# A planned transformer kernel: finer VectorE tasks and another weighing in the plan, and banded attention weights divided on GpSimd by sums from the exponentials

## The chip, the cores and the metric

One of the eight cores of a Trainium2 chip runs the whole program. The metric is the device time of one execution in microseconds (us). A core has TensorE (PE: matmuls, into PSUM), VectorE (DVE), ScalarE (ACT: activation functions from a loaded table), GpSimd (POOL, which works on SBUF alone) and SyncE (SP, which issues DMAs). Each engine runs its own instructions strictly in the order in which they were issued, and waits by semaphore where an operand isn't ready.

## The reference, cut to what matters

Two layers on x of 16 x 256 x 128 floats, all in float32. Layer 0 is softmax attention (stage A: 16 heads of 64) and a routed spline network (stage B). Layer 1 is a mix of linear attention and banded attention (stage C), then causal attention with normalised queries and keys and a mixture of 8 experts (stages D and E). A layernorm follows each. The part whose computation changes is the banded attention, 16 heads of 8, 65 offsets:

```python
s = jnp.einsum('bhsd,bhsd->bhs', qh, ks) * scale + rel_bias[off + WINDOW][None, :, None]
s = jnp.where(valid[None, None, :], s, -jnp.inf)
...
attn = jax.nn.softmax(scores, axis=0)
out, _ = jax.lax.scan(out_step, jnp.zeros_like(qh), (attn, jnp.arange(NWIN)))   # acc + a * vs
```

## The kernel before

The 4096 tokens are cut into 8 groups of 512 (two sequences, four tiles of 128). Each group passes the stages A to E. The code doesn't issue instructions as it walks through the stages: it hands tasks to `Plan.add`, each with its engine (or a choice: "VS" is VectorE or ScalarE), a cost in ns, the buffers that it reads and writes, and an `at`, the group's number plus the stage's offset (0 to 4). `Plan.order` then simulates the engines: again and again it lets that task begin next which can begin soonest, ties broken by `at`. Costs, a lag from one engine to another (`LAG`), a lag on the same engine (`OWN`), 1300 ns for a change of ScalarE's table (`SWITCH`) and 93 for a change of PE's tiling mode (`DRAIN`) are numbers in the code. Buffers come from the classes in `SLOTS`, so many of each; PSUM has four banks `p` and two double banks `s`. The instructions are issued in the order found, engine by engine. So the plan decides which stage of which group stands beside which.

The stages, with the lines of the profile:

- A and D take heads in pairs (`pair`): scores into an `s` bank (PE), the negated maximum (VectorE; line 616 in A; in D mask, two maxima and a scaling, 607, 612, 614), exponentials with their sums from ScalarE's accumulator (634), the reciprocal of the sums (641), the weights times it on GpSimd (647, in place, `pb`), transposes (PE, 662), a copy to `pt` on VectorE or ScalarE (531, 529), and the product with the values.
- B is a long chain of small VectorE instructions on 32 numbers a row, with few matmuls.
- C has, beside the linear attention, eight blocks a group of 64 queries and 96 or 128 keys. For each: the masked queries `qm` (GpSimd, 1031), scores of 16 heads into an `s` bank, bias and maximum (VectorE, 1064, 1065), eight exponentials (1076, `pbC`) without sums, transposes (1082), copies (`ptC`), and 32 matmuls of 64 columns: 16 with the values, spread so that each head has its own columns (`vm`), and 16 with a matrix of ones (`hones`), which give the sums over the keys in the same layout. VectorE then takes the reciprocal of the 64 sums (1109) and multiplies (1110).
- E has 8 experts: four matmuls `h,we` and GELUs each (1346, `hid`), 16 matmuls `we,hid`, and four gated sums into `moe` on VectorE (1361). GELU and exponential lie in different tables. GELUs come in bursts of two experts' (`NBURST`), in which no other ScalarE task with another burst may stand. One task fetches both weights of an expert (1337, 1338).
- A layernorm is three tasks: the statistics of the four tiles (540, 542, VectorE), the root (545, 549, GpSimd), and four scalings (553, VectorE). After stage E come a layernorm, three GpSimd products and sums (`affine`, 927), another layernorm and the DMA out (1368).

Many tasks hold several instructions of one engine, which then follow each other: the four gated sums, the mask, maxima and scaling of a causal pair, the twelve instructions of `rsqrt` (1152 to 1160).

Of the kernel before, what the change touches and what calls it, by code (L numbers as in the profile page):

```python
# [10 lines left out]
I32 = mybir.dt.int32  # L11
AF = mybir.ActivationFunctionType
# [34 lines left out]
    ("ov", 256, 8),  # L47
    ("m", 64, 26),
    ("k1", 256, 4),
    ("b", 512, 2),  # L50
    ("sc", 288, 1),
    ("c", 512, 8),
    ("qm", 512, 2),
    ("pbC", 512, 2),
# [5 lines left out]
    ("e", 512, 1),  # L60
    ("hid", 512, 5),
    ("we", 1024, 2),
# [20 lines left out]

class Plan:

    LAG = {"P": 270.0, "V": 150.0, "S": 170.0, "G": 120.0, "Q": 0.0, "D": 0.0}
    OWN = 80.0
    SWITCH = 1300.0  # L90
    DRAIN = 93.0

# [8 lines left out]
    def add(self, eng, cost, fn, r=(), w=(), at=None, table=None, burst=None, mode="f", hold=()):  # L101
# [9 lines left out]
        for objs, writes in ((r, False), (w, True)):  # L111
            for o in objs:
                o, part = o if isinstance(o, tuple) else (o, None)
                if isinstance(o, Buf):
                    bufs[id(o)] = o
                for q, (writers, readers) in self.state.setdefault(id(o), {}).items():
                    if part is None or q is None or q == part:
                        before.update(writers)
                        if writes:
                            before.update(readers)  # L120
# [23 lines left out]
    def order(self):  # L144
        free = {e: 0.0 for e in "PVSGQD"}
# [17 lines left out]
        while done < len(self.tasks):  # L163
            best = None
            avail = {c: sorted(x for x in v if x is not None) for c, v in slots.items()}
            for e, ts in cand.items():
                pick = None
                for t in ts:
# [3 lines left out]
                    for x, end in t.ready.items():  # L172
                        start = max(start, end + (self.OWN if x == e else self.LAG[x]))
# [65 lines left out]
def kernel(ctx: ExitStack, tc: tile.TileContext, a: dict, out: bass.AP):  # L239
# [231 lines left out]
    hones = ctile("hones", [P, 4, 4 * WD])  # L471

# [7 lines left out]
    def setup_consts():  # L480
# [9 lines left out]
        made((ready_c, "h"), 220, lambda: G.memset(hones, 0.0))  # L490
        for l in range(4):
            made((ready_c, "h"), 60, lambda l=l: G.memset(hones[:, l, l * WD : (l + 1) * WD], 1.0))
# [40 lines left out]
    def layernorm(o, z, name, after=()):  # L533

        mv, rs = W.buf("m", "mv" + name), W.buf("m", "rs" + name)

        def stats():
            st = mv()[:, 8 : 8 + NJ * 6].rearrange("p (j s) -> p j s", s=6)
            for j in range(NJ):
                nc.vector.bn_stats(st[:, j, :], z(J, d=D)[:, j, :])  # L540
            for j in range(NJ):
                nc.vector.bn_aggr(mv()[:, 2 * j : 2 * j + 2], st[:, j, :])

        def root():
            nc.gpsimd.tensor_scalar(
                rs()[:, NJ : 2 * NJ], mv()[:, 0 : 2 * NJ].rearrange("p (j s) -> p j s", s=2)[:, :, 1], EPS, 1.0,
                ALU.add, ALU.mult,
            )
            nc.gpsimd.tensor_tensor(out=rs()[:, 0:NJ], in0=rs()[:, NJ : 2 * NJ], in1=mhalf, op=ALU.pow)

        def scaled():
            for j in range(NJ):
                nc.vector.tensor_scalar(  # L553
                    o(J, d=D)[:, j, :], z(J, d=D)[:, j, :], mv()[:, 2 * j : 2 * j + 1], rs()[:, j : j + 1],
                    ALU.subtract, ALU.mult,
                )

        W.add("V", NJ * (195 + 70), stats, r=[z, *after], w=[mv])
        W.add("G", 1300, root, r=[mv], w=[rs])
        W.add("V", NJ * 257, scaled, r=[z, mv, rs], w=[o])  # L560

# [15 lines left out]
    def pair(pi, qT, kT, v, ov, causal, rq, un=0):  # L577
# [24 lines left out]
        def top():  # L602
            s = sps(S2, a=2)
            n = nmx(n=4, pattern="p (a b) -> p a b", a=2)
            if causal:
                diag = s[:, :, P : 3 * P].rearrange("p a (b k) -> p a b k", k=P)
                nc.vector.tensor_tensor(  # L607
                    out=diag, in0=diag, in1=cmask.unsqueeze(1).unsqueeze(1).to_broadcast([P, 2, 2, P]), op=ALU.add
                )
                for qc in range(2):  # L610
                    c0, nk = col[qc]
                    nc.vector.tensor_reduce(n[:, :, qc], s[:, :, c0 : c0 + nk], AX.X, ALU.max, negate=True)  # L612
                rqp = rq("p (b i m) -> p i m b", n=16, b=2, i=2)[:, pi, 2 * un : 2 * un + 2, :]
                nc.vector.tensor_tensor(out=n, in0=n, in1=rqp, op=ALU.mult)  # L614
            else:
                nc.vector.tensor_reduce(n, s.rearrange("p a (b k) -> p a b k", k=S), AX.X, ALU.max, negate=True)  # L616

        cost = 1790 if causal else dve(1024)
        W.add("V", cost, top, r=[rq] if causal else [], w=[sps, nmx])
# [207 lines left out]
    def stage_b(g):  # L827
# [82 lines left out]
        def add_up():  # L910
            for q, j in enumerate(order):
                V.scalar_tensor_tensor(
                    y(J, d=D)[:, j, :], pv()[:, q, 65:NPAR], mag()[:, q : q + 1], xx(J, d=D)[:, j, :], ALU.mult, ALU.add
                )

        W.add("V", 4 * 259, add_up, r=[pp, mag, xx], w=[y, end_b])
# [5 lines left out]
    def affine(y, gam, bet, xx):  # L922

        nJ = [P, NJ, D]
# [10 lines left out]
    def stage_c(g):  # L935
# [48 lines left out]
        for b in range(2):  # L984
# [24 lines left out]
            def divide(b=b, pn2=pn2, rden=rden):  # L1009
                r = rden()[:, :2]  # L1010
                V.tensor_scalar(r, pn2()[:, :, D], 1e-6, None, ALU.add)
                V.reciprocal(r, r)
                V.tensor_tensor(
                    out=lin(J, d=D)[:, 2 * b : 2 * b + 2, :], in0=pn2()[:, :, :D],
                    in1=r.unsqueeze(2).to_broadcast([P, 2, D]), op=ALU.mult,
                )

            W.add("V", 360 + dve(256), divide, r=[pn], w=[rden, (lin, b)])
# [3 lines left out]
            for i, (w0, w1_) in enumerate(win_of):  # L1022
# [39 lines left out]
                def top(sps=sps, nmx=nmx, nk=nk, t0=t0):  # L1062
                    s8 = sps("p (u k) -> p u k", u=8)[:, :, :nk]
                    V.tensor_tensor(out=s8, in0=s8, in1=band[:, :, t0 : t0 + nk], op=ALU.add)  # L1064
                    V.tensor_reduce(nmx()[:, :8], s8, AX.X, ALU.max, negate=True)  # L1065

                W.add("V", 130 + 2 * dve(8 * nk), top, w=[sps, nmx])
                pts = []
                for half in range(2):
                    pb, pt, tps = W.buf("pbC", "pbC"), W.buf("ptC", "ptC"), W.buf("p", "tpsC")  # L1070

                    def weigh(sps=sps, nmx=nmx, pb=pb, half=half, nk=nk):
                        s8 = sps("p (u k) -> p u k", u=8)
                        for u in range(4):
                            hp = 4 * half + u
                            act(pb("p (u k) -> p u k", u=4)[:, u, :nk], s8[:, hp, :nk], AF.Exp, bias=nmx()[:, hp : hp + 1])  # L1076

                    W.add("S", 4 * (146 + 0.81 * nk), weigh, r=[sps, nmx], w=[pb], table="exp")
# [10 lines left out]
                def values(po=po, pts=pts, vm=vm, nk=nk):  # L1089

                    for what in range(2):
                        for l in range(4):
                            for j in range(4):
                                r = slice(32 * j, 32 * j + 32)
                                h = 4 * j + l
                                c = ((h // 2) % 4) * P + (h % 2) * QC
                                mm(
                                    po()[r, what * QC : (what + 1) * QC],
                                    hones[:nk, l, :] if what else vm[:nk, l, r],
                                    pts[j // 2]()[:nk, c : c + QC],  # L1100
                                    start=l == 0,
                                    stop=l == 3,
                                )

                W.add("P", 1200, values, r=[vt] + pts, w=[po, chain_c[2]], hold=[winT], mode="c32")
                rw = W.buf("m", "rw")

                def divide(po=po, rw=rw, c0=c0):
                    V.reciprocal(rw()[:, :QC], po()[:, QC : 2 * QC])
                    V.tensor_tensor(out=winT()[:, c0 : c0 + QC], in0=po()[:, :QC], in1=rw()[:, :QC], op=ALU.mult)  # L1110

                W.add("V", 700, divide, r=[po], w=[rw, (winT, (b, i))])
# [33 lines left out]
    def rsqrt(o, x, n, eps):  # L1146
# [3 lines left out]
        def go():  # L1150
            V = nc.vector
            V.tensor_scalar(ve(n=n), x(n=n), eps, None, ALU.add)
            yi = y(n=n).bitcast(I32)
            V.tensor_scalar(yi, ve(n=n).bitcast(I32), 1, None, ALU.logical_shift_right)
            V.tensor_scalar(yi, yi, -1.0, float(0x5F3759DF), ALU.mult, ALU.add)
            for k in range(3):
                src, dst = (y, o) if k % 2 == 0 else (o, y)
                V.tensor_mul(u(n=n), src(n=n), src(n=n))
                V.scalar_tensor_tensor(u(n=n), u(n=n), -0.5, ve(n=n), ALU.mult, ALU.mult)
                V.scalar_tensor_tensor(dst(n=n), u(n=n), 1.5, src(n=n), ALU.add, ALU.mult)  # L1160

        W.add("V", 2465 + 12 * (n - 16), go, r=[x], w=[ve, y, u, o])

    def stage_d(g):
# [9 lines left out]
        def half(b, hf):  # L1174
# [13 lines left out]
            for u in range(2):  # L1188
# [12 lines left out]
                def keep(e, ps_q=ps_q, qT=qT, u=u):  # L1201
                    for i in range(2):
# [7 lines left out]
                W.add("VS", (782, 714), keep, r=[ps_q], w=[qT])  # L1210
# [109 lines left out]
    def stage_e(g):  # L1320
# [4 lines left out]
        n = NJ * NE  # L1325
        tg, gT, pb2, moe = W.buf("p", "tg"), W.buf("k1", "gT"), W.buf("p", "pb2"), W.buf("e", "moe")
# [89 lines left out]
```

## Time and profile before

| | |
|---|---|
| median of 3 runs | 2226.43 us (2225.33 to 2226.8) |
| the profiled execution's own time | 2226.4 us |
| its span, first to last instruction | 2224.7 us |
| TensorE busy | 2099.0 us, 94% |
| VectorE busy | 1663.4 us, 75% |
| ScalarE busy | 1308.8 us, 59% |
| GpSimd busy | 784.0 us, 35% |
| mean granted TensorE clock | 0.986 of full |
| ScalarE table loads | 59 of 1.283 us |

"Busy" is the union of an engine's instructions. Matmuls are pipelined, so one that lasts 0.28 us may be followed by the next after 0.11; where it matters, the distance from start to start is used. A stretch is read as start and end in us from the span's start, and a wait as who waited for whom: us in total, times, longest.

### The profile page before, as it was taken

What the parts mean: (1) busy time and instruction counts of PE and PEld (TensorE: products, weight loads), DVE (VectorE), ACT (ScalarE), POOL (GpSimd) and SP (SyncE); (2) the same over time, 40 slices, a digit from 0 to 9 for tenths busy, and PEclk for the clock granted to TensorE, in tenths of its full rate; (3) what the DMA queues carried; (4) which work ended last, traced back from release to release, by engine and by line L of the source; (5) the groups of instructions that cost most, each with busy time, mean ns of one, the idle gap of its engine ahead of it and who ended that gap; (6) DMA issues with size and microseconds to landing.
All of it is one profiled execution on the core that took longest, in us unless ns stands there. A gap on an engine that the chain in (4) does not pass through costs nothing.

```text
span 2224.7 us, 49747 instructions
## 1 busy us (share of the span) xinstructions
PE 2099.0 (94%) x18506; PEld 1563.7 (70%) x18506; DVE 1663.4 (75%) x4784; ACT 1308.8 (59%) x3817; POOL 784.0 (35%) x1413
## 2 busy tenths in 40 slices
PE   8999999999999998999999999999899989989987
PEld 6777777767767766776777767777667667766655
DVE  5788899886688965788757895788856984784742
ACT  4566666764667643676647664666545755654632
POOL 3444362452143621435304360243502530431311
PEclk9999999999999999999999999999999999999998
DMA  5100000000100001000010001100011001101101
GB/s 141 30 1 2 2 1 2 2 2 26 48 15 2 2 29 35 25 2 1 23 41 25 2 1 40 39 6 2 2 43 34 7 2 55 27 1 44 39 20 43
DMA packets 69490, 47.98 MB, mean 22 GB/s; under 512 B 12064, under 2 KB 59904, under 8 KB 69248
## 3 DMA queue, kind: packets, MB, share of 16 engines
q1 hardware_dynamic: 68672, 43.74, 7.3%
q8 instruction: 147, 2.41, 0.5%
q10 hardware_dynamic: 576, 1.05, 0.2%
q14 instruction: 95, 0.78, 0.1%
HBM read 41.89 MB, written 2.88 MB: 20 GB/s over the span
## 4 chain that ended last, share of the span: by engine, by line
PE 53%; DVE 20%; ACT 5%; POOL 2%; issue 2%; POOLq 0%; DVEq 0%; ACTq 0%
PE p L523 39%; PE s L523 6%; PE p L662 4%; DVE m L612 2%; ACT pb L634 2%; PE p L1082 2%; DVE s L607 2%; DVE m L540 1%; DVE m L616 1%; POOL pb L647 1%; DVE x L553 1%; DVE m L614 1%; PE p L1265 1%; DVE uq L1208 1%; DVE s L1064 1%
## 5 line engine op out<-in xcount | busy, mean ns | idle before, releaser
L647 POOL TENSOR_SCALAR pb<-pb,m 128x256 f32<-128x256 f32 (+1 forms) x1024 | 453.8, 460 | 766.9 <-DVE m L641 675.1
L1346 ACT ACTIVATE hid<-p,b 128x512 f32<-128x512 f32 x256 | 170.5, 688 | 304.7 <-PE p L523 290.4
L662 PE MATMUL p<-ident,pb 128*128 128x128 f32 x1792 | 290.0, 282 | 14.1 <-POOL pb L647 5.0
L634 ACT ACTIVATE pb<-s,m,m 128x128 f32<-128x128 f32 (+1 forms) x512 | 257.4, 522 | 61.5 <-DVE m L614 50.7
L634 ACT ACTIVATE pb<-s,m 128x256 f32<-128x256 f32 x512 | 238.8, 490 | 70.5 <-DVE m L616 59.4
L662 PEld LDWEIGHTS p<-ident,pb 128*128 128x128 f32 x1792 | 206.1, 142 | 102.0 <-POOL pb L647 46.8
L523 PE MATMUL p<-h,we 128*128 128x512 f32 x512 | 264.2, 617 | 9.5 <-ACT hid L1346 4.9
L523 PEld LDWEIGHTS p<-we,hid 128*128 128x128 f32 x2048 | 243.3, 194 | 29.9 <-issue 15.7
L523 PE MATMUL p<-we,hid 128*128 128x128 f32 x2048 | 252.8, 279 | 3.9 <-ACT hid L1346 2.1
L529 ACT COPY pt<-p 128x512 f32<-128x512 f32 (+1 forms) x316 | 168.6, 540 | 129.1 <-PE p L662 117.3
L1361 DVE SCALAR_TENSOR_TENSOR e<-p,m,e 128x128 f32<-128x128 f32 x256 | 71.9, 344 | 143.7 <-PE p L523 122.0
L616 DVE TENSOR_REDUCE m<-s 128x4 f32<-128x1024 f32 x128 | 154.7, 1217 | 15.7 <-PE s L523 14.5
L1255 POOL TENSOR_TENSOR kn<-kn,m 128x512 f32<-128x512 f32 x64 | 66.2, 1049 | 283.9 <-DVE m L1160 232.3
L1076 ACT ACTIVATE pbC<-s,m 128x96 f32<-128x96 f32 (+1 forms) x512 | 135.3, 382 | 33.8 <-DVE m L1065 29.3
L523 PE MATMUL s<-ua,ua 64*128 64x256 f32 x1024 | 139.4, 395 | 10.5 <-ACT pb L634 9.0
L523 PE MATMUL s<-ud,uq 64*128 64x128 f32 (+1 forms) x1024 | 118.0, 352 | 21.4 <-ACT pb L634 20.4
L523 PE MATMUL p<-pt,ua 128*64 128x256 f32 x1024 | 136.2, 388 | 1.7 <-ACT pt L529 1.3
L531 DVE COPY pt<-p 128x512 f32<-128x512 f32 (+1 forms) x196 | 120.9, 621 | 20.9 <-PE p L662 19.5
L612 DVE TENSOR_REDUCE m<-s 128x2 f32<-128x256 f32 (+1 forms) x256 | 130.8, 553 | 5.3
L523 PEld LDWEIGHTS p<-h,we 128*128 128x128 f32 x512 | 84.9, 193 | 64.4 <-issue 30.6
L1031 POOL TENSOR_TENSOR qm<-c,hm 128x512 f32<-128x512 f32 x64 | 68.1, 1070 | 153.4 <-PE s L523 132.8
L523 PEld LDWEIGHTS s<-ua,ua 64*128 64x128 f32 x1024 | 91.2, 187 | 39.5 <-ACT pb L634 14.3
(273 smaller groups left out, 4294.0 us busy)
## 6 DMA issues: line engine op xcount, KB each, us to landing
we<-in_L_ffn_w_dram SPq DMA_DIRECT2D x128, 256.0 KB, 2.8
x<-_attn_hidden_states_dram SPq DMA_DIRECT2D x8, 256.0 KB, 2.8
out_dram<-x SPq DMA_DIRECT2D x8, 256.0 KB, 2.3
dpad<-k SPq DMA_DIRECT2D x1, 768.0 KB, 10.3
wq<-in_L_attn_Wq_dram ACTq DMA_DIRECT2D x2, 256.0 KB
wkv<-in_L_attn_Wkv_dram ACTq DMA_DIRECT2D x2, 256.0 KB, 6.8
wkv<-in_L_attn_Wkv_dram SPq DMA_DIRECT2D x2, 256.0 KB, 5.6
wo<-in_L_attn_Wo_dram SPq DMA_DIRECT2D x1, 512.0 KB, 8.4
```

Of the source, the lines that this page charges most:

```text
L523: nc.tensor.matmul(o, lhsT=lhsT, rhs=rhs, start=start, stop=stop)
L529: nc.scalar.copy(o, i)
L531: nc.vector.tensor_copy(o, i)
L612: nc.vector.tensor_reduce(n[:, :, qc], s[:, :, c0 : c0 + nk], AX.X, ALU.max, negate=True)
L616: nc.vector.tensor_reduce(n, s.rearrange("p a (b k) -> p a b k", k=S), AX.X, ALU.max, negate=True)
L634: act(pb()[:, c0 : c0 + nk], s[:, par, c0 : c0 + nk], AF.Exp, bias=nmx()[:, 2 * par + qc : 2 * par + qc + 1], accum_out=sums()[:, 2 * par ...
L647: eng.tensor_scalar(pb()[:, c0 : c0 + nk], pb()[:, c0 : c0 + nk], sums()[:, 2 * par + qc : 2 * par + qc + 1], 1.0, ALU.mult, ALU.mult,)
L662: nc.tensor.transpose(tps()[:, at * P : (at + 1) * P], pb()[:, c0 + kc * P : c0 + (kc + 1) * P], ident)
L1031: (V if e == "V" else G).tensor_tensor(out=qm("p (h q) -> p h q", q=QC), in0=qw()[:, c0 : c0 + QC].unsqueeze(1).to_broadcast(nq), in1=hm8. ...
L1076: act(pb("p (u k) -> p u k", u=4)[:, u, :nk], s8[:, hp, :nk], AF.Exp, bias=nmx()[:, hp : hp + 1])
L1346: W.add("S", 571, lambda ph=ph, hid=hid, ec=ec: act(hid(), ph(), AF.Gelu_apprx_tanh, bias=b1[:, ec : ec + 1]), r=[ph], w=[hid], table="gel ...
L1361: V.scalar_tensor_tensor(m, pe_()[:, j * D : (j + 1) * D], gate()[:, j * NE + e_ : j * NE + e_ + 1], m, ALU.mult, ALU.add)
```

## The change

It has two parts.

The banded weights. Each of the eight exponentials of a block now also writes the sum of its row (`accum_out`). A reciprocal of four sums on VectorE and a product on GpSimd (`pbC` by the reciprocals, four heads at once) divide the weights before they are transposed. The 16 matmuls with ones, the matrix `hones`, the reciprocal of 64 columns and the product behind them are gone; the result is copied from PSUM by VectorE or ScalarE.

The plan. Tasks that held several VectorE instructions are cut into one task each: layernorm statistics and scalings, the causal maxima, the sums of stage B, the division of the linear attention, `rsqrt`, the gated sums. A part of a buffer may now be named by kind, so that parts of different kinds are taken to overlap (`overlap`). `order` computes for each task the longest chain of work behind it, divides it by a weight, takes it off the task's `at`, runs the old procedure (now `line`) with each of ten weights, and keeps the plan whose simulated end is soonest. The lags and some costs have new values. The weights of an expert are fetched by two tasks into buffers of their own. A first GELU matmul of a group now comes after the sum of b2 (`begun`). For the last group alone, the two layernorms and the affine step go tile by tile, the affine step on VectorE, with a DMA out for each tile. Some classes of buffers have a slot more or fewer.

```diff
-    ("ov", 256, 8), ("m", 64, 26), ("k1", 256, 4), ("c", 512, 8), ("qm", 512, 2), ("pbC", 512, 2),
-    ("e", 512, 1), ("hid", 512, 5), ("we", 1024, 2),
+    ("ov", 256, 7), ("m", 64, 30), ("k1", 256, 5), ("c", 512, 7), ("qm", 512, 1), ("pbC", 512, 3),
+    ("e", 512, 2), ("hid", 512, 6), ("w1", 512, 2), ("w2", 512, 2),
...
-    LAG = {"P": 270.0, "V": 150.0, "S": 170.0, "G": 120.0, "Q": 0.0, "D": 0.0}
-    OWN = 80.0
+    LAG = {"P": 265.0, "V": 178.0, "S": 200.0, "G": 60.0, "Q": 0.0, "D": 0.0}
+    OWN = {"P": 0.0, "V": 130.0, "S": 80.0, "G": 80.0, "Q": 0.0, "D": 0.0}
+    RESTS = (1e5, 8e4, 6e4, 5e4, 4e4, 3e4, 2.5e4, 2e4, 1.5e4, 1e4)
...
     def order(self):
+        rest = {}
+        for t in reversed(self.tasks):
+            rest[t.seq] = min(t.cost) + max([self.LAG[t.eng[0]] + rest[n.seq] for n in t.then], default=0.0)
...
+        def again(weight):
+            for t, t.wait, at in first[0]:
+                t.ready, t.end, t.at = {}, None, at - rest[t.seq] / weight
...
+        return again(min(ends)[1])
...
-                            act(pb("p (u k) -> p u k", u=4)[:, u, :nk], s8[:, hp, :nk], AF.Exp, bias=nmx()[:, hp : hp + 1])
+                            act(pb("p (u k) -> p u k", u=4)[:, u, :nk], s8[:, hp, :nk], AF.Exp, bias=nmx()[:, hp : hp + 1],
+                                accum_out=sm()[:, u : u + 1])
+                    W.add("V", 73, lambda sm=sm: V.reciprocal(sm()[:, :4], sm()[:, :4]), w=[sm])
+                    def share(pb=pb, sm=sm, nk=nk):
+                        w4 = pb("p (u k) -> p u k", u=4)[:, :, :nk]
+                        G.tensor_tensor(out=w4, in0=w4, in1=sm()[:, :4].unsqueeze(2).to_broadcast([P, 4, nk]), op=ALU.mult)
+                    W.add("G", gps(4 * nk), share, r=[sm], w=[pb])
...
-                    for what in range(2):
-                                    hones[:nk, l, :] if what else vm[:nk, l, r],
+                            mm(po()[r, :QC], vm[:nk, l, r], pts[j // 2]()[:nk, c : c + QC], start=l == 0, stop=l == 3)
...
-                    V.reciprocal(rw()[:, :QC], po()[:, QC : 2 * QC])
-                    V.tensor_tensor(out=winT()[:, c0 : c0 + QC], in0=po()[:, :QC], in1=rw()[:, :QC], op=ALU.mult)
+                    lambda e, po=po, c0=c0: copy(e, winT()[:, c0 : c0 + QC], po()[:, :QC]), r=[po], w=[(winT, (b, i))],
...
-        W.add("VS", (dve(512), scl(512)), lambda e: copy(e, moe(), pb2()), r=[pb2], w=[moe])
+        W.add("VS", (dve(512), scl(512)), lambda e: copy(e, moe(), pb2()), r=[pb2], w=[moe, begun])
...
-        layernorm(moe, moe, "E1")
-        affine(moe, lngb, lnbb, xx)
-        layernorm(xx, moe, "E2")
+        last = g == NG - 1
+        layernorm(moe, moe, "E1", own=last)
+        affine(moe, lngb, lnbb, xx, own=last)
+        if last:
+            layernorm(moe, moe, "E2", own=True)
```

## The prediction

> **What bounds the kernel now.** I read the page's busy times first, then busy times by stretches of the span, then the waits of TensorE (PE), then its timeline.
>
> ```profile
> span 2224.7 us, 49747 instructions
> ...
> PE 2099.0 (94%) x18506; PEld 1563.7 (70%) x18506; DVE 1663.4 (75%) x4784; ACT 1308.8 (59%) x3817; POOL 784.0 (35%) x1413
> ```
>
> TensorE is busy for all but 125.7 us (2224.7 - 2099.0). About 5.6 of these lie before its first matmul and 15.9 after its last, so some 104 us are gaps on the way. VectorE (DVE) at 75% looks harmless, but 75% is a mean. I cut the span at the first and last gated sum (line 1361) of every group, so that rows alternate between a stage E and what lies between two of them:
>
> ```profile
> core 0: us, PE busy (x) PEld busy (x) DVE busy (x) ACT busy (x) POOL busy (x), PEclk, DMA share, GB/s
> 0.00:530.90 530.90, 507.27 (x4600) 387.14 (x4601) 440.79 (x1189) 324.50 (x1056) 231.80 (x442) 1.00 0.09 20
> 530.90:611.70 80.80, 79.69 (x573) 58.79 (x571) 47.38 (x153) 41.15 (x81) 8.29 (x14) 1.00 0.16 47
> 611.70:803.30 191.60, 183.27 (x1762) 136.59 (x1761) 161.16 (x442) 123.63 (x404) 91.91 (x164) 0.98 0.02 7
> ...
> 1720.40:1839.70 119.30, 106.88 (x1128) 78.98 (x1127) 106.80 (x333) 73.93 (x221) 55.24 (x86) 0.97 0.03 8
> ...
> 2087.30:2157.90 70.60, 61.31 (x411) 41.66 (x410) 47.65 (x151) 38.95 (x122) 30.26 (x61) 0.93 0.03 8
> 2157.90:2209.90 52.00, 49.91 (x278) 35.58 (x276) 8.95 (x33) 18.57 (x27) 0.00 (x0) 1.00 0.20 57
> ```
>
> Columns: stretch, length, busy time of each engine, granted clock, DMA. A stage E spread over 80.8 us leaves PE 99% busy while VectorE does 47 us of other stages' work. Between two of them VectorE is at 84% and PE at 96%. Where both have the same work (1720 to 1840) each reaches 90%: that is what this kernel gets when two engines bind together. The first gated sums stand at 530.9, 803.3, 1084.0, 1344.0, 1628.2, 1839.7, 2017.1 and 2157.9: periods of 272, 281, 260, 284, 211, 177 and 141.
>
> ```profile
> PE s L523 <- ACT pb L634: 30.5, 27, 4.4
> PE p L1265 <- POOL kn L1255: 7.0, 11, 1.2
> PE p L523 <- ACT hid L1346: 7.0, 11, 0.9
> ```
>
> The largest wait of PE is for the score banks (two of them), which the exponentials still read. The long ones cost twice: PEclk is 0.5 for 3.4 to 6.8 us after them, ten times, 51 us in all with 44 of PE busy, so some 22 us are lost to the half clock.
>
> **The change, part by part.**
>
> *No products with ones.*
>
> ```profile
> 200.45 0.65 PE L523 MATMUL p<-ptC,vm 96*32 96x64 f32 x32
> 200.92 0.63 PE L523 MATMUL p<-ptC,hones 96*32 96x64 f32 x32
> 201.48 0.66 PE L662 MATMUL p<-ident,pb 128*128 128x128 f32 x4
> ```
>
> One block of stage C: 16 matmul calls with values and 16 with ones, each with two records (2048 with ones for 64 x 16 calls). Start to start these take 0.47 and 0.56 us. 64 blocks x 0.47 = **30 us off PE** (36 at most); all of it is in stage C, between stage E's.
>
> *What replaces them.* VectorE loses 64 reciprocals of 128x64 (35.1 us) and 64 products (14.4), and gains 128 reciprocals of 4 values (line 641's row: 0.156 each, 0.11 back to back; 14 to 20 us). GpSimd gains 128 products of 384 or 512 elements; the row of qm (128x512, line 1031) says 1.07, so up to 137 us, 784 becomes about 910, 41%. ScalarE gains 512 accumulator reads. No row has this shape with and without; the exponentials of 128 with a read start 0.45 apart (2123.01, 2123.46, 2124.00), eight of 96 without one take 1.96 from 187.85, 0.23 apart. So 0.05 to 0.2 each, 25 to 100 us; I take 60, the nearer row having another operand in it. Against that the built order has 32 table loads for 59: 27 x 1.283 = 35 us less. ScalarE stays near 60%. It also has 91 pt copies moved from ScalarE to VectorE (0.62 each, 56 us), and some 15 us of other copies. VectorE so ends 2 to 3% higher than before, not lower. The longer way from scores to transposes (exponentials +0.8, reciprocal 0.2, product 1.1) is covered: the order puts at least 8 us of PE work between a block's scores and its second transposes (3.3 before).
>
> *The new order.* I took both programs' instruction order as built (it holds no times) and priced each matmul by its start-to-start row, and each VectorE instruction by its own; before, this gives 2017 us for PE and 1647 for VectorE, near the 1663 measured. Two things come out.
>
> First, scores. A score bank is free again some 3.6 us after A's scores and 4.3 after D's (2120.85 to 2125.14 in the timeline). Before, 29 of 254 rewrites of a bank come with less PE work than that behind the last, short by 35 us in sum (30.5 measured as wait); after, 8, short by 3.5. This wait should nearly go, and most half-clock stretches with it: 30 plus about 15 us.
>
> Second, and against it: **stage E is now one block**. All 32 GELUs of a group follow each other on ScalarE with no exponential between (before: 8 to 24 at a time). Between first and last gated sum VectorE is left only 11.4 us of work, where it had 45 to 70, and PE has 54.6 us. So the rest of VectorE's work must fit between the blocks: priced, **199 us of VectorE against 194 of PE** in each of the first three intervals, 194 against 182, then 136 against 111, 109 against 97, 68 against 66. VectorE becomes the bound there, and the 30 us of PE saved lie where PE no longer binds.
>
> *Sum*, from 0, with VectorE 93% busy between blocks (between the 90% above and the 97% of the best slice of 55.6 us, 1723.6 to 1779.2 with 53.73; I lean upward since the chains of short instructions, 12 in a row in the rsqrt at 0.2 each, may now be mixed with others):
> - to the first gated sum: 15 us more PE work stands ahead of it (511 for 496), 531 + 15/0.955 = 547, less 6 of the 23 us of gaps there: 541
> - four periods: 199/0.93 = 214 three times and 209, plus four blocks of 55.5: 1073
> - three periods: 136/0.93 = 146, 109/0.93 = 117, and 75 (stage D alone; 70.6 before for 6% less work), plus blocks of 55, 55 and 58: 506
> - the last stage E and its end: 66.8 before, 4 less: 63
>
> The 4 us of the end:
>
> ```profile
> 2208.80 1.13 DVE L1361 SCALAR_TENSOR_TENSOR e<-p,m,e 128x128 f32<-128x128 f32 x4 [5.34 <-PE p L523]
> ...
> 2213.59 1.26 POOL L927 TENSOR_TENSOR e<-e,lngb 128x512 f32<-128x512 f32 x1 [1.23 <-DVE e L553]
> 2214.93 1.26 POOL L927 TENSOR_TENSOR e<-e,lnbb 128x512 f32<-128x512 f32 x1
> 2216.28 1.26 POOL L927 TENSOR_TENSOR e<-e,x 128x512 f32<-128x512 f32 x1
> ...
> 2221.33 0.38 SPq L1368 DMA_DIRECT2D out_dram<-x  x1
> ```
>
> By tiles, the three GpSimd products (4.0 us) become twelve VectorE ones of about 0.25 (3 us, the first under PE's last matmuls), but two roots become eight at up to 1.2 us, 9.6 in a row. Bounds 0 and 7 saved; 4 is the middle. The moved b2 sum ahead of stage E makes PE wait for the gate, 2 us once, within the 75.
>
> 541 + 1073 + 506 + 63 = 2183; the profiled execution's time lies 1.7 over its span (2226.4, 2224.7), and the median is the same 2226.4, so **2185 us**, 1.9% less.
>
> **The rivals.**
> - *VectorE binds harder* (slower). The mechanism is the one above at 88% busy: PE stands idle between blocks, its gaps bring the half clock back. Intervals of 226 (three times), 220, 155, 124, 80 give 548 + 1120 + 526 + 65 + 2 = 2261. It decides from 90%: there the sum is 2230. For it: 90% is the best of any long stretch so far. Against: score rewrites are better spaced, and finer tasks let VectorE pass over what isn't ready when the order is made. 0.15.
> - *PE keeps the bound.* If VectorE reaches 97%, 205 us an interval, PE at 194 needs as much (194/0.957 = 203): 535 + 1037 + 492 + 62 + 2 = 2128. For it: the best slice. 0.20.
> - *The plan does nothing*: periods as they were, the ones gone, the end shorter: 2226 - 30 - 4 = 2192. Told from the forecast by periods of 268 with stage E spread; the order speaks against it. 0.05.
> - *GpSimd's new products hold VectorE up.* Line 614 has a median of 0.164 but a mean of 0.243 and a maximum of 1.29 us; line 553 (z<-z, scalars) 0.35 and up to 1.33: at 184.74 a VectorE product of two SBUF tiles takes 1.21 us beside a GpSimd product that runs until 185.40. The excess of these rows sums to 30 us over 784 of GpSimd, 4%; 137 more would cost 5, which I count as inside the 93%. If each held VectorE for its whole 1.05, that were 130 us, 2185 + 130 = 2315; half of it 2250. 0.05 for 2230 and over. The Trainium skill, SBUF — State Buffer, section Who interferes with whom, states the hard form: a VectorE instruction with two SBUF inputs and a GpSimd one that reads SBUF lock each other out whole. By that rule the trace's long ones agree, and the sum would go by how many meet.
>
> **How the numbers follow.** Forecast 0.52 (own range 2150 to 2222), PE bound 0.20, plan without effect 0.05, VectorE bound 0.15, lock 0.05, the rest 0.03. A measurement tells 0.2%, 4.5 us, from no change. Within it fall 0.02 each of the forecast's upper end and the slower rival's lower one and the rest's 0.03: 0.07. Slower: 0.13 and 0.05, 0.18. Faster: 0.50, 0.20 and 0.05, 0.75. The range 2115 to 2250 leaves out the bottom of the second rival and the top of the slower ones, 2 in 10.
>
> **What would show it.** Cut at the gated sums: blocks of about 55 us with VectorE at 11, and intervals of 205 to 220 with VectorE at 90% or more. PE's wait for pb under 10 us; new PE waits for VectorE (pt, ua, ud copies, maxima) in its place. Wrong if the intervals come under 200 (VectorE's rows then cost less when mixed) or over 222, or if PE's waits for GpSimd's pbC pass 10 us.

## The result, and the profile after

The changed kernel takes **2166.3 us** (median of 4 runs, 2164.62 to 2167.57) against 2225.9: ratio 0.973 with a 95% interval of 0.9715 to 0.9749, 59.6 us less. The forecast was 2185 (41 less). The profiled execution took 2164.62 us. From its page, the busy times and VectorE's row of tenths:

```profile
span 2162.9 us, 46331 instructions
...
PE 2054.3 (95%) x16458; PEld 1538.4 (71%) x16458; DVE 1618.9 (75%) x4928; ACT 1286.1 (59%) x4234; POOL 897.5 (41%) x1545
...
DVE  6789899899298983989558894789828964963842
```

TensorE's gaps sum to 108.6 us (125.7 before); of the 61.8 us that the span lost, 17.1 are gaps and 44.7 TensorE's busy time. VectorE's total fell by 44.5 us, and its row of tenths now drops to between 2 and 5 where a stage E stands and is 8 or 9 between. Cut at the first and last gated sum of each group (columns as before: stretch, length, the engines' busy times, clock, DMA):

```profile
core 0: us, PE busy (x) PEld busy (x) DVE busy (x) ACT busy (x) POOL busy (x), PEclk, DMA share, GB/s
0.00:545.70 545.70, 521.32 (x4282) 397.95 (x4286) 471.98 (x1330) 336.85 (x1195) 267.45 (x477) 1.00 0.09 19
545.70:598.80 53.10, 52.05 (x331) 37.97 (x332) 11.43 (x44) 23.41 (x48) 2.28 (x5) 1.00 0.26 75
598.80:800.50 201.70, 199.03 (x1740) 152.32 (x1739) 185.66 (x568) 137.48 (x484) 109.13 (x185) 1.00 0.02 5
...
1627.60:1771.00 143.40, 130.07 (x1119) 95.31 (x1119) 129.34 (x411) 89.54 (x315) 76.89 (x119) 0.95 0.02 5
...
2007.10:2101.00 93.90, 78.54 (x546) 55.22 (x545) 64.76 (x208) 49.93 (x154) 35.24 (x71) 0.91 0.03 7
```

Blocks of 53 us with VectorE at 11.4, then stretches of 202 to 207: the shape is the forecast's. Its filling is not. In the first three long stretches VectorE has 186 us of work, not 199, and is 91 to 92% busy, while PE is 99% busy; in the fourth (207.4 us) VectorE is at 89% and PE at 93%. In the late ones neither engine is near full: the last is 93.9 long with PE at 78.5. The gated sums now begin at 545.7, 800.5, 1056.9, 1313.2, 1573.7, 1771.0, 1949.1 and 2101.0.

PE's waits:

```profile
PE s L554 <- ACT pb L682: 13.1, 18, 1.6
PE p L1322 <- POOL kn L1312: 7.4, 8, 3.3
PE p L710 <- POOL pb L695: 6.4, 15, 2.5
...
PE p L1150 <- POOL pbC L1144: 0.8, 4, 0.2
```

The wait for a score bank fell from 30.5 to 13.1, its longest from 4.4 to 1.6. The wait for the new GpSimd product is nearly nothing. Up to PE's last matmul PEclk is 0.5 for 51.2 us, as much as before. But 44.4 of it now lies after 1560 us (37.6 before), 6.8 in the four long periods ahead (13.6).

The new instructions, from the groups of the three engines (busy us, mean ns | idle before):

```profile
L1136 ACT ACTIVATION_READ_ACCUMULATOR pbC<-s,m 128x1 f32 x512 | 117.4, 229 | 0.0
...
L1140 DVE RECIPROCAL m<-m 128x4 f32<-128x4 f32 x128 | 21.4, 167 | 26.2 <-ACT pbC L1136 26.1
...
L1144 POOL TENSOR_TENSOR pbC<-pbC,m 128x384 f32<-128x384 f32 (+1 forms) x128 | 119.5, 936 | 226.7 <-DVE m L1140 192.4
```

The 117.4 us of the first row are not what the sums cost ScalarE, since each read overlaps the exponential before it. Eight exponentials of 96 before, and the first ones of a block in the changed kernel:

```profile
187.85 1.96 ACT L1076 ACTIVATE pbC<-s,m 128x96 f32<-128x96 f32 x8 [0.25 <-DVE m L1065]
```

```profile
619.12 0.34 ACT L1136 ACTIVATE pbC<-s,m 128x96 f32<-128x96 f32 x1 [0.73 <-DVE m L1126]
619.36 0.19 ACT L1136 ACTIVATION_READ_ACCUMULATOR pbC<-s,m 128x1 f32 x1
619.45 0.33 ACT L1136 ACTIVATE pbC<-s,m 128x96 f32<-128x96 f32 x1
```

From start to start (medians) they are 0.316 us apart for 0.223, those of 128 0.342 for 0.250: 0.093 a read, 47 us for the 512, and 0.4 for four exponentials.

### The profile page after: what moved, and what is told of

It is laid out like the page before. It is cut to its first block, busy times and chain, and to the rows that moved or that the text cites. A ratio compares the mean times of both kernels' runs of the same rounds, so it can differ in the third digit from the quotient of the medians.

```text
span 2162.9 us, 46331 instructions
## 1 busy us (share of the span) xinstructions
PE 2054.3 (95%) x16458; PEld 1538.4 (71%) x16458; DVE 1618.9 (75%) x4928; ACT 1286.1 (59%) x4234; POOL 897.5 (41%) x1545
## 4 chain that ended last, share of the span: by engine, by line
PE 61%; DVE 24%; POOL 6%; ACT 5%; issue 3%; DMA 0%; POOLq 0%; DVEq 0%; ACTq 0%
PE p L554 44%; PE s L554 8%; PE p L710 5%; POOL pb L695 3%; DVE m L653 3%; ACT pb L682 2%; DVE m L663 2%; DVE pt L562 2%; DVE s L644 2%; PE p L1150 1%; DVE s L1121 1%; PE p L1322 1%; DVE m L1126 1%; DVE kn L562 1%; DVE m L1297 1%
## 5 line engine op out<-in xcount | busy, mean ns | idle before, releaser
L682 ACT ACTIVATE pb<-s,m,m 128x128 f32<-128x128 f32 (+1 forms) x512 | 255.6, 517 | 33.5 <-DVE m L659 26.8
L682 ACT ACTIVATE pb<-s,m 128x256 f32<-128x256 f32 x512 | 237.1, 486 | 63.7 <-DVE m L663 56.7
L554 PEld LDWEIGHTS p<-w,hid 128*128 128x128 f32 x2048 | 239.0, 192 | 26.6 <-issue 23.7
L554 PE MATMUL p<-h,w 128*128 128x512 f32 x512 | 240.8, 608 | 5.1 <-ACT hid L1406 3.8
L554 PE MATMUL p<-w,hid 128*128 128x128 f32 x2048 | 242.2, 275 | 0.9
L1144 POOL TENSOR_TENSOR pbC<-pbC,m 128x384 f32<-128x384 f32 (+1 forms) x128 | 119.5, 936 | 226.7 <-DVE m L1140 192.4
L562 DVE COPY pt<-p 128x512 f32<-128x512 f32 (+1 forms) x287 | 173.0, 612 | 14.5 <-PE p L710 13.6
L1136 ACT ACTIVATE pbC<-s,m 128x96 f32<-128x96 f32 (+1 forms) x512 | 173.8, 376 | 15.3 <-DVE m L1126 14.3
L554 PEld LDWEIGHTS p<-h,w 128*128 128x128 f32 x512 | 92.9, 194 | 99.9 <-issue 79.4
L663 DVE TENSOR_REDUCE m<-s 128x4 f32<-128x1024 f32 x128 | 154.5, 1214 | 11.0 <-PE s L554 10.5
L560 ACT COPY pt<-p 128x384 f32<-128x384 f32 (+1 forms) x225 | 116.1, 540 | 68.3 <-PE p L710 61.4
L653 DVE TENSOR_REDUCE m<-s 128x2 f32<-128x512 f32 (+1 forms) x256 | 132.6, 545 | 1.0
L1136 ACT ACTIVATION_READ_ACCUMULATOR pbC<-s,m 128x1 f32 x512 | 117.4, 229 | 0.0
```

The lines of the kernel that those rows point to most:

```text
L554: nc.tensor.matmul(o, lhsT=lhsT, rhs=rhs, start=start, stop=stop)
L560: nc.scalar.copy(o, i)
L562: nc.vector.tensor_copy(o, i)
L653: lambda qc=qc, c0=c0, nk=nk: nc.vector.tensor_reduce(nm()[:, :, qc], sps(S2, a=2)[:, :, c0 : c0 + nk], AX.X, ALU.max, negate=True),
L663: lambda: nc.vector.tensor_reduce(nm(), sps(S2, a=2).rearrange("p a (b k) -> p a b k", k=S), AX.X, ALU.max, negate=True),
L682: act(pb()[:, c0 : c0 + nk], s[:, par, c0 : c0 + nk], AF.Exp, bias=nmx()[:, 2 * par + qc : 2 * par + qc + 1], accum_out=sums()[:, 2 * par ...
```

## The experiments

Differences in the last column are between medians; the kernel before was run beside each (its medians 2225 to 2228), so they are good to some 3 us.

| kernel | median us | ratio to before, 95% | to the changed kernel |
|---|---|---|---|
| banded weights alone, old plan | 2304.3 | 1.0337 to 1.0368 | +138.0 |
| those, new weighing and lags | 2265.8 | 1.0163 to 1.0193 | +99.5 |
| all but the banded weights | 2173.9 | 0.9752 to 0.9781 | +7.6 |
| no weighing | 2273.6 | 1.0191 to 1.0236 | +107.3 |
| old lags | 2223.0 | 0.9979 to 0.9998 | +56.7 |
| old numbers of buffers | 2212.3 | 0.9920 to 0.9954 | +46.0 |
| another of the ten weights | 2202.6 | 0.9876 to 0.9910 | +36.3 |
| VectorE's tasks whole again | 2176.1 | 0.9760 to 0.9789 | +9.8 |
| 29 us more on PE | 2184.9 | 0.9806 to 0.9842 | +18.6 |
| 27 us more on VectorE | 2187.5 | 0.9816 to 0.9846 | +21.2 |
| both | 2205.3 | 0.9892 to 0.9922 | +39.0 |
| GpSimd's product twice | 2213.0 | 0.9926 to 0.9955 | +46.7 |

**One half of the change at a time.** The kernel before with the new banded weights (and four more `m` buffers), planned by the old procedure:

```diff
-    ("m", 64, 26),
+    ("m", 64, 30),
...
+                            act(..., bias=nmx()[:, hp : hp + 1], accum_out=sm()[:, u : u + 1])
+                    W.add("G", gps(4 * nk), share, r=[sm], w=[pb])
...
-                    for what in range(2):
```

> The kernel before with the new banded weights alone (sums from the exponentials, division on GpSimd, no products with ones; 30 scalar buffers for 26), planned by the old procedure. If TensorE's work sets the time, 30 us less of it give 2226 - 30 = 2196 us, 2190 to 2205. If the gain of the change lies in the plan and the longer way from scores to transposes eats what the ones gave, 2215 to 2235.

Both expectations missed: it is 78 us *slower* than the kernel before. Its waits:

```profile
PE s L519 <- ACT pb L630: 26.2, 31, 3.5
PE s L519 <- ACT pbC L1072: 19.8, 17, 4.5
...
PE p L658 <- DVE pt L527: 11.9, 13, 1.0
```

Thirty us of matmuls are gone, but PE is idle for 192.3 us (125.7 before) and at half clock for 129.7 (51.2). The score banks now wait for stage C's exponentials too: 19.8 us, where it was 1.0. That these hold the banks longer because of their sums is argued: four take only 0.4 us more.

The opposite, the changed kernel with the old banded weights:

```diff
-                    for l in range(4):
+                    for what in range(2):
+                        for l in range(4):
...
+                                    hones[:nk, l, :] if what else vm[:nk, l, r],
```

> The changed kernel with the old banded weights (products with ones, reciprocal of 64 sums and product on VectorE), planned by the new procedure. If the two parts add, 2166 + 30 = 2196 us (2188 to 2202), half of the gain. If the new plan needs the lighter stage C, 2205 or more; if the ones cost nothing under it since VectorE binds, 2166 to 2176.

2173.9, in the third range: the plan alone brings nearly all, and the banded weights 7.6 us. The 16 calls with ones do cost PE time there: from the first matmul with `ptC` of a block to the next other matmul, 64 blocks take 69.9 us in sum, against 37.2. So 32.6 us left PE and 7.6 left the time; PE's whole busy time is 2058.9 us here and 2054.3 in the changed kernel, so other matmuls took some 28 us more. Part of that is known: half clock lasts 27.3 us in this kernel and 51.2 in the changed one, with PE busy for 23.7 and 44.8, which is about 11 us of work. The rest stays open. Against the kernel before (2099.0) PE's busy time fell by 40 us with the same matmuls. About 10 of these are half clock; PE also changes from one kind of product to another 1987 times for 2315. What brings the other 30 isn't shown.

**Which part of the plan.** All task weights off (a single one, so large that the correction vanishes):

```diff
-    RESTS = (1e5, 8e4, 6e4, 5e4, 4e4, 3e4, 2.5e4, 2e4, 1.5e4, 1e4)
+    RESTS = (1e15,)
```

> The changed kernel planned with one weight so large that the work behind a task counts for nothing: finer tasks, new lags, new buffers and new banded weights stay. As built, the GELUs of a group come in runs of 8 and 24 instead of 32. If weighing the work behind makes the gain of the plan: 2205 to 2260 us. If finer tasks or the lags make it: 2160 to 2180.

2273.6, above the first range, and 47 us slower than the kernel before. Half clock is at 119.5 us, GELUs stand 8 to 24 in a row up to the last group, there are 46 table loads for 32, and the score-bank wait is

```profile
PE s L554 <- ACT pb L682: 53.7, 47, 3.4
```

The old lags:

```diff
-    LAG = {"P": 265.0, "V": 178.0, "S": 200.0, "G": 60.0, "Q": 0.0, "D": 0.0}
+    LAG = {"P": 270.0, "V": 150.0, "S": 170.0, "G": 120.0, "Q": 0.0, "D": 0.0}
```

(and `OWN` 80 throughout)

> The changed kernel planned with the lags of before (PE 270, VectorE 150, ScalarE 170, GpSimd 120, 80 on the own engine for each). If a plan that fits the chip's real lags better carries the gain: 2190 us or more, with PE's waits for ScalarE's exponentials back above 25 us. If the lags hardly matter: 2160 to 2180.

2223.0, with a score-bank wait of 27.1 us, as the first expectation said: 57 us from some tens of ns in a table. That the new lags lie nearer to the chip's isn't shown by it, only that the plan made with them is better.

VectorE's tasks joined as before:

> The changed kernel with the VectorE tasks joined again as before (layernorm statistics and scalings, maxima, rsqrt, the sums of B, gated sums), all else new; the last group's tile by tile end stays. As built, the GELUs still come 32 in a row. If mixing short dependent VectorE instructions with others is what brought VectorE's work between the blocks from 199 priced to 186 us: VectorE at 195 to 200 there, intervals of 212 or more, 2205 to 2235 us. If finer tasks are incidental: 2160 to 2180.

Its diff gives `layernorm`, the maxima of D and C, the sums of B, the division in C, `rsqrt`, the scaled copies to `uq` and the gated sums their old single tasks. 2176.1, 10 us, a small part; the signs of the first expectation (195 to 200 us of VectorE in intervals of 212) did not come: 176.5 in the first three, 196 to 197 long, with blocks of 64. But it shows what the finer tasks do for VectorE: its total, 1618.1, is the changed kernel's, with 202 copies to `pt` on VectorE for 287. The finer tasks pay for some 43 us of copies (156.1 less 113.3, each counted from the end of the instruction before it) by putting independent instructions between dependent ones. Over all kinds of instruction of which both kernels have as many, the changed kernel spends 60.5 us less so counted; this kernel spends 3.8 more than the one before. The maximum of 128x256 that follows its mask takes 424 ns (median) in this kernel and the one before, 331 in the changed one, where another instruction stands between; the product with the scales 164 and 73. In sums, the products of line 659 and their like (200 in all) take 35.1 us for 48.6, the maxima 332.6 for 348.4, line 1216's squares 14.5 (112 with their like) for 27.5.

The banded weights on the old kernel, now with the new procedure, its ten weights and its lags, but whole tasks, old buffers, one fetch for both weights of an expert, and the old end:

> The kernel e1 (before, with the new banded weights) planned by the new procedure with its weights and lags, tasks as coarse and buffers as few as before. e1 took 2304 us. If the old procedure is what couldn't place the longer way through stage C: 2180 to 2220. If the coarse tasks or the buffers are: 2260 to 2310.

2265.8, so the new procedure takes back 38 us of 138, and 100 stay. That is in the second range. Its first gated sum begins only at 626.0 us, and it loads tables 72 times. Part of these 100 is in the buffers:

```diff
-    ("ov", 256, 7), ("k1", 256, 5), ("c", 512, 7), ("qm", 512, 1), ("pbC", 512, 3), ("e", 512, 2), ("hid", 512, 6),
+    ("ov", 256, 8), ("k1", 256, 4), ("c", 512, 8), ("qm", 512, 2), ("pbC", 512, 2), ("e", 512, 1), ("hid", 512, 5),
```

> The changed kernel with the numbers of buffers of the kernel before (ov 8, k1 4, c 8, qm 2, pbC 2, e 1, hid 5); m stays at 30 for the sums and w1, w2 at 2 each; the plan is made anew and still has 32 GELUs in a row. Theory (the gain is the plan's weighing and lags; buffers are a detail): within 15 us of the changed kernel, 2160 to 2180. Rival (the third block of pbC and the sixth of hid are what lets the longer chain of stage C and the dense stage E go; they explain most of the 100 us that weighing and lags left undone on the old kernel): 2200 or more, with waits of PE for pbC or hid of over 10 us.

2212.3, the rival's side. In its waits the score bank waits for stage C's exponentials, as in the kernel with the banded weights alone (1.0 us in the changed kernel):

```profile
PE s L554 <- ACT pbC L1136: 12.3, 14, 2.2
PE p L554 <- DVE ptC L562: 9.9, 12, 2.1
```

In ScalarE's waits these exponentials wait 6.9 us, 9 times, for transposes that still read a `pbC` block (0.8, twice, in the changed kernel).

Then a plan from the same list, one that the procedure didn't choose:

```diff
+    RESTS = (2.5e4,)
```

> The changed kernel with the plan of weight 2.5e4 instead of the 4e4 that the procedure picks out of its ten: same instructions except for ScalarE's table loads (43 for 32), GELUs in runs of 16, 8 and 8 in the first four groups and of 32 in the last four. Theory (the weighing itself is what helps, by keeping long chains ahead, and the neighbouring weight does nearly as well): 2165 to 2190, blocks of the first four groups near 65 us and intervals shorter by what the blocks take. Rival (the dense stage E is what helps; splitting it costs as it did without weighing): 2210 or more, the loss in the first four groups.

2202.6, between the two. The first gated sum begins 19.2 us later (564.9), the first three periods are 7 to 8 us longer each, and the other four together no longer than in the changed kernel. So 19 us of the loss come ahead of any block and some 20 with the four split ones: these blocks take 24 us more each, the stretches behind them 15 to 26 less.

**Which engine binds.** The changed kernel, same order, with 16 more matmuls a block, whose output nobody reads:

```diff
+                    for l in range(4):
+                        for j in range(4):
...
+                            mm(po()[r, QC : 2 * QC], vm[:nk, l, r], pts[j // 2]()[:nk, c : c + QC], start=l == 0, stop=l == 3)
```

> The changed kernel, same order and same plan, with 16 more matmuls in each of the 64 blocks behind the product with the values (into columns that nothing reads): 30 us more work for TensorE where the ones stood. Theory 'TensorE kept the bound between the stage E blocks' (it is 98.7% busy there in the first intervals): +24 to +32 us, 2190 to 2198. Theory of the prediction, 'VectorE binds there': under +10, 2166 to 2176.

and with a reduction of 3 x 128 a block on VectorE, not read either:

```diff
+                        V.tensor_reduce(spare[:, :3], band[:, :3, :], AX.X, ALU.max),
```

> The changed kernel, same order and same plan, with one more VectorE reduction of 384 elements a row (about 0.47 us, from a constant into a spare tile) behind the maximum of each of the 64 blocks of stage C: 30 us more work for VectorE. 'VectorE binds between the blocks': +24 to +35 us, 2190 to 2200. 'TensorE kept the bound': under +12, 2166 to 2178.

Both lie between the theories. Their first long stretch, PE's load first, then VectorE's (columns as above):

```profile
605.50:809.60 204.10, 201.63 (x1960) 155.51 (x1961) 185.83 (x568) 137.40 (x484) 109.11 (x185) 1.00 0.02 5
```

```profile
606.20:810.70 204.50, 199.82 (x1740) 152.48 (x1740) 189.21 (x576) 137.60 (x484) 109.12 (x185) 1.00 0.02 5
```

PE's load is 29.4 us (the 64 stretches with `ptC` grow from 37.2 to 66.7) and costs 18.6; VectorE's busy time grows by 26.6 and the time by 21.2. Neither engine alone is the bound. In the first long period (254.7 us, full clock in all these runs) there are 3.7 us of PE's load or 3.3 of VectorE's, and each makes it 257.6. Both loads together tell whether they share one slack:

> The changed kernel in the same order with both loads of the two runs before: 16 more matmuls for each block of stage C (about 30 us of PE) and a reduction of 3 times 128 for each (about 30 us of VectorE). What they write is not read. Alone they cost 18.6 and 21.2 us. Theory 1 (each engine binds in stretches of its own, so that costs add): plus 40, 2200 to 2212. Theory 2 (both bind in the same stretches, and what one load costs already gives the other room): plus 25 to 33, 2190 to 2199.

39.0 for 18.6 + 21.2: the costs nearly add, so each engine binds mostly at places of its own. That they match so well is in part the clock's doing: PE is at half clock for 51.2 us without a load, 41.0 with its own, 54.6 with VectorE's and 61.4 with both. In the first long period, at full clock, both loads cost 5.1 us (259.8), where they cost 2.9 each alone.

**GpSimd against VectorE.** A second product behind each division, times one, in place:

```diff
+                        G.tensor_tensor(out=w4, in0=w4, in1=ones1.unsqueeze(2).to_broadcast([P, 4, nk]), op=ALU.mult)
```

> The changed kernel in the same order with a second GpSimd product behind each of the 128 divisions (the same 384 or 512 elements, times one, in place): GpSimd's busy time rises by some 120 us to about 1017, and each block's chain by 0.94. Theory (GpSimd's products hold up VectorE little; the waits for pbC are covered by the order): 2166 to 2175, VectorE's busy time up by less than 6 us. Rival (the two engines lock each other out of SBUF): VectorE's busy time up by 30 us or more, and the time by 20 or more (2187 and over).

2213.0, the rival's side; VectorE's busy time rises by 21.3 us, between the two. Two things happen, and how the 46.7 us divide between them isn't shown. PE now waits for the product:

```profile
PE p L1151 <- POOL pbC L1145: 26.8, 44, 1.5
```

(0.8 us, 4 times, in the changed kernel). And VectorE is held up. Its timeline:

```profile
1889.24 1.04 POOL L1144 TENSOR_TENSOR pbC<-pbC,m 128x512 f32<-128x512 f32 x1
1889.31 4.29 DVE L592 TENSOR_SCALAR e<-e,m,m 128x128 f32<-128x128 f32 x4
1890.36 1.04 POOL L1145 TENSOR_TENSOR pbC<-pbC,ones 128x512 f32<-128x512 f32 x1
1891.36 1.04 POOL L1144 TENSOR_TENSOR pbC<-pbC,m 128x512 f32<-128x512 f32 x1
1892.48 1.04 POOL L1145 TENSOR_TENSOR pbC<-pbC,ones 128x512 f32<-128x512 f32 x1
```

Four scalings with a median of 0.35 us take 4.29, one for each of GpSimd's products. The same is in the changed kernel, with the one product:

```profile
661.68 1.04 POOL L1144 TENSOR_TENSOR pbC<-pbC,m 128x512 f32<-128x512 f32 x1 [0.21 <-DVE m L1140]
661.82 0.94 DVE L1217 SCALAR_TENSOR_TENSOR m<-m,m 128x32 f32<-128x32 f32 x1
```

Between the two kernels the order is the same, so rows compare one to one: the scalings `e<-e` rise from 13.5 to 17.8 us, `x<-e` from 10.5 to 15.3, the integer steps and products of `rsqrt` (1211 to 1218) by about 8; copies from PSUM (`pt`, 98.6) and the statistics (28.9) don't change. The Trainium skill, SBUF — State Buffer, section Who interferes with whom, states it so: VectorE contends with a GpSimd instruction that reads SBUF when both of its own inputs lie in SBUF, and with GpSimd when a copy or tensor_scalar runs in a two-port mode; then one of them waits for the other's whole instruction. The rows agree in kind.

## Why the prediction was right, and where it was not

- **Sum and sign.** Right: faster, within the forecast's own range, 19 us below its number. That it came so near is partly luck, since errors cancel: the first four long stretches took 35 us less than forecast, the blocks 12 less, the three late stretches 24 more and the start 5 more. The sum's terms: first gated sum 545.7 (541), first three stretches 202 to 203 (214), the fourth 207 (209), blocks 53 to 58 (55 to 58), late stretches 143, 125, 94 (146, 117, 75), last block and end 62 (63).
- **"VectorE becomes the bound there, and the 30 us of PE saved lie where PE no longer binds."** Failed. The 199 us of VectorE were priced with the old order's rows, in which chains of dependent instructions follow each other; in the new order 186 were needed, 13 us a stretch less, and PE was 99% busy there. The instructions of the first long stretch, at what each kind cost before, counted from the end of the instruction before it, come to 199.7 us; so counted they took 185.8. PE's 194 were priced low as well: 199 to 201 were measured, and the same pricing gave 2017 us before for 2099.0 busy. The run with 29 us put back on PE costs 18.6 in the same order; under a plan made anew taking off the ones was worth 7.6. So little of the saving reached the time, as said, but VectorE alone is not the reason. The rival that PE keeps the bound had this part, but not its 97% of VectorE, and its 2128 was missed by the late stretches and the start.
- **"VectorE so ends 2 to 3% higher than before."** Failed, the same error of size: 2.7% lower, though the copies moved to it as said (196 to 287 of `pt`).
- **The late stretches.** The forecast took 93% of VectorE and 75 us for stage D alone; 361.8 us were measured for 338. Neither engine is full there (PE 84 to 91%, VectorE 69 to 90%), and 41 us of the half clock lie in these stretches, with PE busy for 34.8, so some 17 us of its time. The term of 75 was too small from the start: it took the last stretch for 6% more work than the 70.6 us before, but by the rows shown PE has 546 matmuls for 411 and VectorE 64.8 us for 47.7.
- **"This wait should nearly go, and most half-clock stretches with it."** Half right: 30.5 to 13.1 us (under 10 was asked for), and the half clock did not shrink, it moved to the end. The terms of 30 and 15 us don't stand in the sum, which goes by VectorE; the half clock that stayed shows in the late stretches.
- **The end.** 4 us saved were forecast, from last gated sum to end 14.8 fell to 13.1, 1.7 us. The roots on one element take 0.55 us where four took 1.02, so eight for two undo most of the affine step's gain:

```profile
2151.03 0.55 POOL L586 TENSOR_TENSOR m<-m,mhalf 128x1 f32<-128x1 f32 x1
```

- **ScalarE, GpSimd.** Near 60% and 41%: right. The reads of the accumulator cost 0.093 us each and 47 in sum, within the bounds of 0.05 and 0.2, for the 60 taken. The table loads went to 32, and ScalarE stayed off the bound.
- **GpSimd's products cost 5 us, "which I count as inside the 93%".** Too small. The second product cost VectorE 21.3 us for 121 of GpSimd, 18%, where 4% was taken. By the same rate the change's own product costs VectorE about 20 us (estimate; the first product alone wasn't taken away in this order). The rival needed 45 us or more for 2230, so a third of each product. It priced one product; the second one cost the time 46.7, part of it through PE's wait.
- **"At least 8 us of PE work" covers the longer chain of stage C.** Right for the order as made (0.8 us of wait), but with little to spare: 0.94 us more per product brought 26.8 us of wait.

Where the gain comes from, then: not from the work that was taken off PE. Under the old plan it lost 78 us, under the new one it gains 7.6. It comes from the order, and the parts of the plan don't add: taken out singly, weighing, lags and buffers cost 107, 57 and 46 us, more than the whole gain of 60. Without the weighing PE waits 53.7 us for score banks, with the old lags 27.1, in the changed kernel 13.1; the third `pbC` buffer goes with the longer chain. Each cost was measured, but on one plan each, and any number that is altered gives another plan. How far plans scatter without any cause in the part altered wasn't measured, and the one neighbour tried cost 36 us. So 57 and 46, and less likely 107, may in part be such scatter. That it is the third `pbC` among the seven buffer numbers is argued from the waits. Not tried: the two weight fetches, the sum of b2 ahead of stage E, and the old end, each by itself; and what a plan that knows GpSimd's doubled product would make of it.

## What to carry to other kernels

Where an order is fixed ahead of time, an edit and its order are one change: try the edit under a plan made anew, and don't judge either by itself. Price an engine's work in a new order by what instructions cost beside independent neighbours, and when two engines are both above 90%, look at both: here an us added to either in the same order cost 0.6 to 0.8, while 32.6 us taken off one, with the plan made anew, gave 7.6. Keep GpSimd's long SBUF products away from VectorE's SBUF-to-SBUF instructions, and count a share of them as VectorE's.

## What the runs showed of the hardware

- A VectorE scaling of 128x128 from SBUF to SBUF, 0.34 us, took up to 1.2 beside GpSimd products of 1.04; copies from PSUM and statistics beside the same products kept their times.
- An accumulator read after an exponential has a record of 0.229 us on ScalarE, but moved the next exponential by 0.093 (0.223 to 0.316 from start to start at 128x96, 0.250 to 0.342 at 128x128).
- A VectorE maximum of 128x256 took 424 ns behind the masking whose result it reads and 331 with another instruction between, each counted from the end of the one before.
- GpSimd's power took 1.02 us for four values a partition and 0.55 for one.
- PE's clock stretches at 0.5 came in steps of 3.4 us (3.4, 6.8, 10.2, 13.7, 20.5) up to the last matmul of each of the fourteen kernels; the changed kernel has 17 us fewer gaps than the one before and the same 51.2 us at half clock.
